# Moving the first products of four expert tiles into the attention stage of a two-layer gated transformer kernel, and making the tile lists in three parts

## The chip, the core and the metric

The kernel runs on one core of a Trainium2 chip (trn2). The metric is the device time of one execution in microseconds (us), and the figure of a kernel is the median of its runs. Engines are named as the profile names them: PE is TensorE (matrix products; PEld is its weight load), DVE is VectorE, ACT is ScalarE, POOL is GpSimd and SP is SyncE. Each works through its own queue of instructions in order, and an instruction that waits holds up all that stand behind it in that queue.

## What is computed

The reference is two layers, each of a cross-attention and a feed-forward part, on `x` of 4 batches of 512 tokens of width 256, all in float32. Only the last part matters for the change:

```python
x = x + tanh(g_xattn[0]) * attn0(layernorm(x), ctx)      # 16 heads of width 16, decay by distance
x = x + tanh(g_ffn[0])   * ffn0(layernorm(x))            # 256 -> 1024 -> 256, weights made ternary
x = x + tanh(g_xattn[1]) * attn1(layernorm(x), ctx)      # 16 heads, relu of q, k, v
x = x + tanh(g_ffn[1])   * ffn1(layernorm(x))
# ffn1, for h of 2048 tokens:
expert_idx = argmax(h @ W_router)                        # one of 4 experts for each token
hidden = gelu(h @ W1[expert_idx] + b1[expert_idx])       # 256 -> 1024
y = layer_norm(hidden @ Wo + bo + h) * ln_gamma + ln_beta
```

## The kernel before

**Attention.** A unit is one tile of 128 rows of one head group (four heads). There are 32 head groups (2 layers x 4 batches x 4) and so 128 units. In each unit PE makes four score products `pm` whose row maxima DVE takes (`maxima`, L504), six units ahead (`LEAD`), and four products `psc` of keys with shifted queries that ACT turns into exponentials (`weights`, L519). Each is a 32 x 128 by 32 x 512 product; four of them stand beside each other in the array. Every fourth unit PE multiplies the exponentials of a head group with the values (`weighted`, `po`, L547), and two units later it turns the maxima (`pmT`) and the last output (`pn`), which DVE divides and adds to `x`. All results of PE pass through eight PSUM banks that are handed out in turn (`bank_psum`): a product waits until the product eight places before it was read out by ACT or DVE.

**What fills the units.** Everything else of a layer is cut into jobs that stand in chains: a job has a cost in us of PE and a gap in units to the one before, and a chain has a first and a last unit. `slot(u)` runs after the scores of unit u: it takes due jobs, and others as long as their cost fits into `SLOT` = 3.1 us. Jobs are the projections of the next batch (`project`, `prepare`), the first feed-forward part (`ffn0`) and `route(b)`: the norm of the batch, its rows to a DRAM buffer `rows_d` (two DMAs on SP), the router's product `plT`, one-hot choice and the rank of each token within its expert (`ranks`, `prk`).

**The expert part** works on 19 tiles of 128 rows that hold tokens of one expert each. `dispatch(second)` makes a list: from ranks and counts DVE computes the place of each token (`lists`, `token_places`, `by_tile`), makes selection matrices (`picked`, `sel`, 128 x 512), and `gathered` multiplies them on PE (`pid_d`, L881: for each token tile a 128 x 128 weight load and a product of 9 or 10 columns) to get the token index of each row. The result goes to `get`, `put` and `wrow`, the index lists of the DMAs. The first list covers three batches and 9 tiles (`T_FULL`) and is made in the last units of attention; the second covers the rest and 10 tiles, and is made between the first tiles.

For a tile j, `fetch_rows` and `fetch_weights` (L918, L930) gather its rows and its 1 MB of expert weights by indirect DMAs that POOL issues. `turn_tile` (`ptx`, L1040) transposes the rows, ACT or DVE copies them to `xs`. `hidden_tile` (`pg`, L1101) makes the first product in two halves and ACT applies gelu out of PSUM (L1107). `output_tile` (`pyf`, L1117) makes the second product, `norm_tile` is the layer norm on DVE with one power on POOL (L1132), and `put_tile` (L1144) writes the rows out with an indirect DMA from POOL.

Only tile 0 is turned in attention, in the last unit. After attention the order is written out by hand: `hidden_tile(0)`, `weighted` of the last head group, tile 1 turned, `divided` of the last group, the weights of tiles 2 and 3, the norm of the last batch, and then for each j `hidden_tile(j)`, `turn_tile(j + 1)`, `put_tile(j - 2)`, `output_tile(j - 1)`, `norm_tile(j - 1)` and the fetches of tile j + 3. `early` and `late` name the steps of the last batch's routing and of the second list that stand between.

Of the kernel before, what the change touches and what calls it, by code (L numbers as in the profile page):

```python
# [19 lines left out]
P = 128  # L20
# [12 lines left out]
T_FULL = 9  # L33
T_ALL = TT + NE - 1
LEAD = 6
# [9 lines left out]
def flamingo_kernel(ctx: ExitStack, tc: tile.TileContext, t: dict, out: bass.AP):  # L45
# [727 lines left out]
    def dispatch(second):  # L773

        tiles = (TT, T_ALL - T_FULL) if second else ((B - 1) * NT, T_FULL)
        K, T = tiles
        j0 = T_FULL if second else 0
        nm = f"d{int(second)}"
# [7 lines left out]

        def lists():
# [3 lines left out]
            if second:  # L791
                nc.vector.tensor_tensor(left, count[:, K, :], taken, ALU.subtract)
            else:
                nc.vector.tensor_scalar(left, count[:, K, :], float(1 - P), None, ALU.add)
# [10 lines left out]
            nc.vector.tensor_reduce(ends, part, AX.X, ALU.add)  # L805
            first = ends[:, 0:NE]
            if second:
                first = small([NE], "first")
                nc.vector.tensor_tensor(first, ends[:, 0:NE], taken, ALU.subtract)
            else:  # L810
                nc.vector.tensor_scalar(ends, ends, float(P * T), None, ALU.min)
                nc.vector.tensor_tensor(taken, ends[:, 1 : NE + 1], ends[:, 0:NE], ALU.subtract)
            st.update(ends=ends, first=first)

        def token_places():
# [5 lines left out]
            if second:  # L821
                nc.vector.tensor_tensor(
                    ok, at, across(ends[:, 0:NE].unsqueeze(1), K, NE), ALU.is_ge
                )
            else:
                nc.vector.tensor_tensor(
                    ok, at, across(ends[:, 1 : NE + 1].unsqueeze(1), K, NE), ALU.is_lt
                )
            nc.vector.tensor_tensor(ok, ok, onehot[:, 0:K, :], ALU.mult)
# [5 lines left out]
        def by_tile():  # L835

            ends, place1 = st["ends"], st["place1"]
            ge = small([TT, T_ALL - T_FULL + 1], "ge")[:, 0:K, 0 : T + 1]
# [4 lines left out]
            tid = small([TT, T_ALL - T_FULL], "tid")[:, 0:K, 0:T]  # L843
# [5 lines left out]
            st.update(tid=tid, row1=row1)  # L849

        def by_expert():

            ends = st["ends"]
            past = small([T_ALL - T_FULL, NE - 1], "past")[:, 0:T, :]
# [4 lines left out]
            ex = small([T_ALL - T_FULL], "ex")[:, 0:T]  # L859
# [5 lines left out]
        def picked(k0):  # L865
            def run():
                pool, tag, bufs = (act, "oT", 2) if second else (wts, "xg", 4)
                sel = pool.tile([P, 4, P], F32, tag=tag, name=f"sel_{nm}{k0}", bufs=bufs)
# [8 lines left out]
        def gathered(k0):  # L877
            def run():
                pid = bank_psum(f"pid_{nm}{k0}")[:, 0:T]
                for k in range(4):  # L880
                    nc.tensor.matmul(  # L881
                        pid, lhsT=st["sel", k0][:, k, :], rhs=st["tid"][:, k0 + k, :],
                        start=(k == 0), stop=(k == 3),
                    )
                if k0 == 0:
                    st["pid"] = small([T_ALL - T_FULL], "pid")[:, 0:T]
                    nc.vector.tensor_copy(st["pid"], pid)
                else:
                    nc.vector.tensor_tensor(st["pid"], st["pid"], pid, ALU.add)
                if k0 + 4 == K:  # L890

                    nc.vector.tensor_scalar(
                        get[:, j0 : j0 + T], st["pid"], 1.0, -1.0, ALU.max, ALU.add
                    )
                    none = small([T_ALL - T_FULL], "none")[:, 0:T]
                    nc.vector.tensor_scalar(
                        none, st["pid"], 0.0, float(2 * B * S), ALU.is_equal, ALU.mult
                    )
                    nc.vector.scalar_tensor_tensor(
                        put[:, j0 : j0 + T], st["pid"], -1.0, none, ALU.add, ALU.add  # L900
                    )

            return run

        return (
            [(lists, 0, 0), (token_places, 0, 0), (by_tile, 0, 0)],
            [(picked(k), 0, int(k == 0)) for k in range(0, K, 4)],
            [(by_expert, 0, 1)],
            [(gathered(k), 1.0, int(k == 0)) for k in range(0, K, 4)],
        )  # L910

# [3 lines left out]
    def fetch_rows(j):  # L915
        have = (B if j >= T_FULL else B - 1) * S
        xg[j] = wts.tile([P, 2 * D], F32, tag="xg", name=f"xg{j}", bufs=4)
# [6 lines left out]
    def fetch_weights(j):  # L924

        if j % 5 < 2:
# [7 lines left out]
        )  # L934

# [26 lines left out]
    for layer in range(2):  # L962
# [21 lines left out]
    fetches = [  # L984
        (lambda j=j, f=f: f(j), 0, 0)
        for f, j in (
            (fetch_rows, 0), (fetch_weights, 0), (fetch_rows, 1), (fetch_weights, 1), (fetch_rows, 2),
            (fetch_rows, 3),
        )
    ]  # L990
    for b in range(B - 1):
        u0 = first_unit(1, b + 1)
        if b < B - 2:
            chain(route(b), u0 + 4, u0 + 13)
        else:
            heads, *rest = dispatch(False)
            heads[0] = (heads[0][0], 0, 0)
            chain([*route(b), *heads, *sum(rest, []), *fetches], u0 + 2, n_units - 5)
# [36 lines left out]
    xs, hs, ys = {}, {}, {}  # L1035

    def turn_tile(j):
# [231 lines left out]
```

## Time and profile before

| what | value |
|---|---|
| runs | 866.21, 863.21, 866.26 us; median 866.21 us |
| profiled execution, its own time | 865.25 us |
| its span, first to last instruction | 863.2 us, 13527 instructions |
| PE, DVE, ACT, POOL busy | 832.9, 555.2, 418.2, 271.7 us |
| mean granted TensorE clock | 0.985 |
| start of the last product with the values (`po`), end of the last `pyf` | 705.43 us, 852.84 us |

The profile is one execution; times in it count from its first instruction. It gives groups of equal instructions with their total, the chain of work that ended last followed back from the end, the order of instructions in time, and for chosen stretches the busy time of each engine with the granted clock of PE. Ends of products are modelled and they overlap, so a busy PE need not be at its peak: what a product costs is read from the start of one group of products to the start of the next. Each float32 product is recorded twice, so `x32` is 16 products.

### The profile page before, as it was taken

What the parts mean: (1) busy time and instruction counts of PE and PEld (TensorE: products, weight loads), DVE (VectorE), ACT (ScalarE), POOL (GpSimd) and SP (SyncE); (2) the same over time, 40 slices, a digit from 0 to 9 for tenths busy, and PEclk for the clock granted to TensorE, in tenths of its full rate; (3) what the DMA queues carried; (4) which work ended last, traced back from release to release, by engine and by line L of the source; (5) the groups of instructions that cost most, each with busy time, mean ns of one, the idle gap of its engine ahead of it and who ended that gap; (6) DMA issues with size and microseconds to landing.
All of it is one profiled execution on the core that took longest, in us unless ns stands there. A gap on an engine that the chain in (4) does not pass through costs nothing.

```text
span 863.2 us, 13527 instructions
## 1 busy us (share of the span) xinstructions
PE 832.9 (96%) x5222; PEld 472.6 (55%) x5222; DVE 555.2 (64%) x1192; ACT 418.2 (48%) x876; POOL 271.7 (31%) x435
## 2 busy tenths in 40 slices
PE   6999999999999999999999999999999999999995
PEld 3444444435463346445554445644444558999994
DVE  6778778766857784768646865577777615644443
ACT  2475565553555452655445563357566353233331
POOL 5536455524342422311100120012002035445542
PEclk9999999999999999999999999999999799999998
DMA  9100000000001000000000010001001046556650
GB/s 315 60 1 1 1 1 2 1 1 0 2 13 25 1 1 0 26 1 1 1 1 25 1 50 1 1 1 50 1 1 49 1 147 226 165 173 201 196 190 14
DMA packets 17775, 42.01 MB, mean 49 GB/s; under 512 B 2158, under 2 KB 12144, under 8 KB 15280
## 3 DMA queue, kind: packets, MB, share of 16 engines
q0 software_dynamic: 5168, 27.08, 9.5%
q1 hardware_dynamic: 12128, 13.54, 4.7%
q8 instruction: 41, 0.67, 0.3%
q10 hardware_dynamic: 416, 0.54, 0.2%
q14 instruction: 22, 0.18, 0.1%
HBM read 34.86 MB, written 6.68 MB: 48 GB/s over the span
## 4 chain that ended last, share of the span: by engine, by line
PE 74%; DVE 9%; issue 8%; POOL 5%; DMA 2%; ACT 1%; POOLq 0%; ACTq 0%; DVEq 0%
PE pm L490 15%; PE po L547 13%; PE psc L490 13%; PE ph L660 7%; PE py_f L375 7%; PE pk L447 4%; PE pva L416 4%; DVE m L504 4%; PE pq L447 3%; PE pmT L561 2%; PE py_wo L375 2%; DMA out_dram<-y,put 2%; POOL out_dram L1144 2%; POOL wg L930 2%; POOL rstd_y L1132 1%
## 5 line engine op out<-in xcount | busy, mean ns | idle before, releaser
L504 DVE TENSOR_REDUCE m<-pm 128x1 f32<-128x512 f32 x512 | 316.6, 682 | 106.3 <-PE psc L490 103.5
L519 ACT ACTIVATE p<-psc 128x512 f32<-128x512 f32 x512 | 267.6, 602 | 164.3 <-PE psc L490 161.1
L490 PE MATMUL psc<-q,k 32*128 32x512 f32 x1024 | 286.6, 635 | 2.1 <-DVE m L504 1.9
L490 PE MATMUL pm<-k,q 32*128 32x512 f32 x1024 | 266.8, 618 | 2.6 <-DVE m L504 1.7
L522 POOL TENSOR_TENSOR p<-p,dec 128x256 f32<-128x256 f32 x128 | 93.4, 734 | 179.1 <-ACT p L519 179.1
L490 PEld LDWEIGHTS pm<-k,q 32*128 32x128 f32 x1024 | 95.7, 185 | 87.7 <-issue 51.4
L490 PEld LDWEIGHTS psc<-q,k 32*128 32x128 f32 x1024 | 108.6, 186 | 55.5 <-issue 25.2
L547 PE MATMUL po<-p,v 128*32 128x512 f32 x1024 | 117.0, 597 | 1.9 <-DVE m L504 1.9
L1107 ACT ACTIVATE ha<-pg,wg 128x128 f32<-128x128 f32 x152 | 43.2, 369 | 89.1 <-PE pg L1101 83.3
L547 PEld LDWEIGHTS po<-p,v 128*32 128x32 f32 x1024 | 31.8, 110 | 83.5 <-issue 62.6
L1101 PE MATMUL pg<-xs,wg 128*128 128x128 f32 x608 | 71.2, 276 | 1.4 <-DVE xn_f L356 1.4
L1101 PEld LDWEIGHTS pg<-xs,wg 128*128 128x128 f32 x608 | 70.5, 192 | 3.3 <-issue 1.7
L1117 PE MATMUL pyf<-wo,ha 128*128 128x256 f32 x304 | 68.6, 379 | 0.0
L615 POOL TENSOR_TENSOR x<-x,o 128x256 f32<-128x256 f32 x14 | 10.2, 729 | 174.8 <-DVE o L608 142.9
L1117 PEld LDWEIGHTS pyf<-wo,ha 128*128 128x128 f32 x304 | 56.4, 190 | 6.8
L660 PE MATMUL ph<-xTf,w1q 128*128 128x512 f32 x128 | 60.0, 605 | 0.0
L553 ACT COPY oT<-po 128x512 f32<-128x512 f32 x32 | 18.7, 585 | 80.3 <-PE po L547 80.3
L375 PE MATMUL py_f<-w2q,h 128*128 128x256 f32 x256 | 57.2, 382 | 0.0
L375 PEld LDWEIGHTS py_f<-w2q,h 128*128 128x128 f32 x256 | 48.1, 190 | 9.3 <-DVE m L504 3.0
L1121 DVE TENSOR_TENSOR y<-y,pyf 128x256 f32<-128x256 f32 x19 | 8.0, 421 | 53.8 <-PE pyf L1117 53.5
L447 PE MATMUL pk<-cT,wk 128*128 128x512 f32 x68 | 35.1, 641 | 7.3 <-DMA cT<-in_ctxT_dram 7.3
L660 PEld LDWEIGHTS ph<-xTf,w1q 128*128 128x128 f32 x128 | 22.6, 190 | 30.4 <-issue 18.1
(204 smaller groups left out, 797.8 us busy)
## 6 DMA issues: line engine op xcount, KB each, us to landing
x<-in_x_dram SPq DMA_DIRECT2D x4, 512.0 KB, 8.6
rows_d<-xn_f SPq DMA_DIRECT2D x4, 512.0 KB, 3.0
rows_d<-x SPq DMA_DIRECT2D x4, 512.0 KB, 3.5
cT<-in_ctxT_dram SPq DMA_DIRECT2D x3, 512.0 KB, 9.6
w1q<-in_w_dram SPq DMA_DIRECT2D x1, 1024.0 KB, 8.8
w2q<-in_w_dram SPq DMA_DIRECT2D x1, 1024.0 KB, 11.2
wo<-in_wo_dram SPq DMA_DIRECT2D x2, 512.0 KB, 3.8
rows<-in_rows_dram SPq DMA_DIRECT2D x1, 640.0 KB, 9.1
```

Of the source, the lines that this page charges most:

```text
L375: nc.tensor.matmul(py[:, n, :], lhsT=operand(c, n0 + n), rhs=w[:, c, :], start=(c == 0), stop=(c == chunks - 1),)
L416: nc.tensor.matmul(pv[:, ts(n, D)], lhsT=cT[b][:, c, ts(n0 + n, P)], rhs=wv[:, c, :], start=(c == 0), stop=(c == NC - 1),)
L447: nc.tensor.matmul(pp, lhsT=attn_w[layer][w][:, c, ts(tt, P)], rhs=src[:, c, :], start=(c == 0), stop=(c == NC - 1),)
L490: nc.tensor.matmul(out_, lhsT=lhs[r, ts(n, P)], rhs=rhs[r, :], start=True, stop=True)
L504: nc.vector.tensor_reduce(m[:, n, 2 * pair + i, r : r + 1], pm[i], AX.X, ALU.max)
L519: nc.scalar.activation(p[:, i, :], psc[i], AF.Exp, scale=SCALE)
L522: nc.gpsimd.tensor_tensor(d, d, dec.unsqueeze(1).to_broadcast([P, 2, P]), ALU.mult)
L547: nc.tensor.matmul(po[i * HP : (i + 1) * HP, :], lhsT=v_sb[b % 2][0][:, kt, c0 : c0 + HP], rhs=ps_exp[NT * s + kt, i // 2][:, i % 2, :], s ...
L660: nc.tensor.matmul(ph, lhsT=w1q[:, c, ts(f, P)], rhs=st["xT"][:, c, :], start=(c == 0), stop=(c == NC - 1),)
L1101: nc.tensor.matmul(ph[:, f, :], lhsT=w[:, c, ts(f2 * NF // 2 + f, P)], rhs=xs[j][:, c, :], start=(c == 0), stop=(c == NC - 1),)
L1107: nc.scalar.activation(ha[:, f, :], ph[:, f, :], AF.Gelu, bias=wg[j][:, NC * FF + fa : NC * FF + fa + 1],)
L1117: nc.tensor.matmul(py, lhsT=hs[j, f // 4][:, f % 4, :], rhs=wo1[f // 4][:, f % 4, :], start=(f == 0), stop=(f == NF - 1),)
```

## The change

There are now three lists instead of two (`LISTS`): two batches and tiles 0 to 4, three batches and tiles 5 to 8, four batches and tiles 9 to 18. The first is made as soon as batch 1 is routed, in the third batch's units of layer 1 and the first of the fourth's; the second in the last six units of attention; the third between tiles as before. Four tiles (`T_AHEAD`) have rows and weights fetched within attention, are turned there and have their first product made there, all but the second half of tile 3. These steps are jobs of a chain, with costs 0.3 and twice 1.75. Their results are only copied out of PSUM, by ACT for tiles 0 to 2 and by DVE for tile 3; the bias is kept by a copy on POOL, and gelu runs after attention from SBUF to SBUF (`activated`). The rows of tiles 0, 1 and 2 are fetched a second time for the residual.

The token indices are no longer gathered by products with 128 x 128 weights. `collected` takes the index matrix (padded to 32 columns, set to zero on POOL) as weights and the selection as the moving side, four token tiles at a time in column strips of the array. The result is copied by ACT, transposed by PE and summed by DVE over the four strips (`tokens`). In a list after the first, DVE has up to five more small instructions.

After attention the order is a queue: second half of tile 3, gelu of tile 0, the last `weighted`, tile 4 turned, last `divided`, the norm of the last batch, then the fetches of rows 5, 3, 6, 7 and weights 5, 6, 7 on POOL. On PE follow the first product of tile 4, the turning of tile 5, the second products of tiles 0 to 3 with the last batch's routing between, the first product of tile 5, and then second product of j and first product of j + 2 in turn. Tile 9, the first of the last list, is turned just before the second product of tile 8, and tile 10 is turned right before its own first product.

```diff
-T_FULL = 9
+LISTS = ((2, 0), (3, 2 * NT - NE + 1), (4, 3 * NT - NE + 1))
+T_LIST = T_ALL - LISTS[-1][1]
+T_AHEAD = 4
...
+            tid = space("tid").rearrange("p (k w) -> p k w", w=HP)
+            nc.gpsimd.memset(tid, 0.0)
...
-        def gathered(k0):
-            def run():
-                pid = bank_psum(f"pid_{nm}{k0}")[:, 0:T]
-                for k in range(4):
-                    nc.tensor.matmul(
-                        pid, lhsT=st["sel", k0][:, k, :], rhs=st["tid"][:, k0 + k, :],
-                        start=(k == 0), stop=(k == 3),
-                    )
...
+        def collected():
+
+
+            pT = bank_psum(f"pidT_{nm}")[:, 0:P]
+            for k in range(K):
+                nc.tensor.matmul(
+                    pT[k % 4 * HP : (k % 4 + 1) * HP, :], lhsT=st["tid"][:, k, :],
+                    rhs=st["sel", k - k % 4][:, k % 4, :], start=(k < 4), stop=(k >= K - 4),
+                )
+            st["pT"] = const.tile([P, P], F32, tag="dec", name=f"pT_{nm}")
+            nc.scalar.copy(st["pT"], pT)
+
+        def tokens():
+            pp = bank_psum(f"pid_{nm}")[:, 0:P]
+            nc.tensor.transpose(pp, st["pT"], ident)
+            pid = small([T_LIST], "pid")[:, 0:T]
+            nc.vector.tensor_reduce(
+                pid, pp.rearrange("p (i t) -> p t i", i=4)[:, 0:T, :], AX.X, ALU.add
+            )
...
+    def turn_tile(j):
...
+        copy = nc.vector.tensor_copy if j == T_AHEAD else nc.scalar.copy
+        copy(xs[j], pt.rearrange("p (c n) -> p c n", c=NC))
+
+    def hidden_half(j, f2):
...
+        if j < T_AHEAD:
+            ha = wts.tile([P, S], F32, tag="h", name=f"ha{j}{f2}", bufs=8)
+            if f2 == 0:
+                biases[j] = sml.tile([P, NF], F32, tag="b1", name=f"b1_{j}")
+                nc.gpsimd.tensor_copy(biases[j], b1)
...
+        if j < T_AHEAD:
+            (nc.scalar.copy if j < T_AHEAD - 1 else nc.vector.tensor_copy)(ha, ph)
+        else:
+            activated(j, f2, ph)
...
+            turn_0, *rest_0 = tile_steps(0)
+            ahead = chain(
+                [
+                    *route(b), *dispatch(0), step(fetch_rows, 0), step(fetch_weights, 0),
+                    step(fetch_rows, 1), step(fetch_weights, 1), step(fetch_rows, 2),
+                    step(fetch_rows, 3), (turn_0[0], turn_0[1], 2), *rest_0, step(fetch_rows, 4),
+                    step(fetch_weights, 2, gap=1), *tile_steps(1), step(fetch_rows, 0),
+                    step(fetch_weights, 3, gap=1), *tile_steps(2), step(fetch_rows, 1),
+                    step(fetch_weights, 4, gap=1), *tile_steps(3)[:2],
+                ],
+                u0 + 3, n_units - 1,
+            )
...
+            routed = chain(route(b), u0 + 2, u0 + 9)
+            chain(dispatch(1), n_units - LEAD, n_units - 1, routed)
...
-    hidden_tile(0)
+    hidden_half(T_AHEAD - 1, 1)
+    fetch_rows(2)
+    for f2 in range(2):
+        activated(0, f2)
     weighted(last)
-    turn_tile(1)
+    turn_tile(T_AHEAD)
     divided(last)
...
+    steps = {
+        ("o", 1): [turn3], ("o", 2): [products3], ("o", 3): [logits3],
+        ("h", 5): [ranks3, lists, token_places, by_tile], ("o", 4): [*sels, by_expert],
+        ("h", 6): [collected], ("o", 5): [tokens],
     }
...
+    first = LISTS[-1][1]
+    queue = [("h", 4), *(("o", j) for j in range(4)), ("h", 5)]
+    for j in range(4, T_ALL - 2):
+        queue += [("o", j), ("h", j + 2)]
+    queue.remove(("o", first - 1))
+    queue.insert(queue.index(("h", first)), ("o", first - 1))
+    queue += [("o", T_ALL - 2), ("o", T_ALL - 1)]
+    for j in (5, 3, 6, 7):
+        fetch_rows(j)
+        if j > 3:
+            fetch_weights(j)
+    for kind, j in queue:
+        if kind == "h":
+            for f2 in range(2):
+                hidden_half(j, f2)
+            if j + 1 < T_ALL and j + 1 != first:
+                turn_tile(j + 1)
+        else:
+            if j + 1 == first:
+                turn_tile(first)
+            if j < 3:
+                for f2 in range(2):
+                    activated(j + 1, f2)
+            output_tile(j)
+            norm_tile(j)
+            if j > 0:
+                put_tile(j - 1)
```

## The prediction, made before the changed kernel ran

> **What bounds the kernel now.** I read the page first: PE is busy for 832.9 of 863.2 us, so only what PE does, or waits for, near the end can matter. Then the granted clock in short stretches, the order of instructions in time, and the DMA table. The stretches (columns: us; PE, PEld, DVE, ACT, POOL busy; clock; DMA share; GB/s):
>
> ```profile
> 675.00:680.00 5.00, 3.13 (x12) 1.17 (x8) 4.62 (x18) 2.65 (x6) 0.00 (x0) 0.96 0.01 2
> 680.00:685.00 5.00, 5.00 (x18) 2.08 (x16) 4.61 (x11) 1.19 (x2) 0.73 (x1) 0.50 0.00 0
> 685.00:690.00 5.00, 5.00 (x28) 4.99 (x24) 0.34 (x2) 2.06 (x4) 0.00 (x0) 0.50 0.00 0
> 690.00:695.00 5.00, 5.00 (x34) 1.58 (x37) 0.58 (x4) 2.06 (x4) 3.28 (x3) 0.67 0.36 80
> ```
>
> PE runs at half clock from about 679.6 to 693.3 (0.96 and 0.67 give the ends), just where the first list is made. The order in time says why:
>
> ```profile
> 677.99 2.48 DVE L504 TENSOR_REDUCE m<-pm 128x1 f32<-128x512 f32 x4
> 678.73 2.43 PE L490 MATMUL psc<-q,k 32*128 32x512 f32 x4 [1.87 <-DVE m L504]
> 680.39 1.88 DVE L869 TENSOR_TENSOR sel_d<-from_one,row_d 128x512 f32<-128x512 f32 x3
> 685.01 5.29 PE L881 MATMUL pid_d<-tid_d,sel_d 128*128 128x9 f32 x24
> ```
>
> DVE did 3.8 us of list arithmetic (674.18 to 677.99) ahead of the maxima, PE ran out of PSUM banks, and the index products then took 5.22 us at half clock. After attention the bound is PE alone, with one DMA wait at tile 2:
>
> ```profile
> 709.77 0.66 PE L598 MATMUL pn<-ident,oT 128*128 128x128 f32 x4 [0.34 <-ACT oT L553]
> 712.73 1.02 POOL L930 DMA_INDIRECT wg<-in_w1e_dram,wrow  x1 [12.02 <-DVE st_f L321]
> 717.41 0.20 POOL L336 TENSOR_TENSOR rstd_f<-rstd_f,fix_f 128x4 f32<-128x4 f32 x1
> 719.04 3.81 PE L1101 MATMUL pg<-xs,wg 128*128 128x128 f32 x32 [1.36 <-DVE xn_f L356]
> ...
> 838.53 0.38 PE L1040 MATMUL ptx<-ident,xg 128*128 128x128 f32 x2
> 838.75 3.62 PE L1117 MATMUL pyf<-wo,ha 128*128 128x256 f32 x16
> 842.20 3.73 PE L1101 MATMUL pg<-xs,wg 128*128 128x128 f32 x32
> 845.77 7.07 PE L1117 MATMUL pyf<-wo,ha 128*128 128x256 f32 x32
> ```
>
> The DMA table gives the time from issue to landing (last column, median us):
>
> ```profile
> xg<-rows_d,get POOLq DMA_INDIRECT x19, 3.6
> wg<-in_w1e_dram,wrow POOLq DMA_INDIRECT x19, 6.6
> ```
>
> The wait at 719.04 is for the weights issued at 712.73, which land 6.0 us later; the norm's last row only ends beside it. Start to start, a tile in the steady part is 3.57 (`pg`), 0.22 (`ptx`), 3.46 (`pyf`): 7.25 us with no gap. Moving 3.57 us of PE work into attention gains only what attention hides; PE's work as a whole stays. So I add up two parts: attention from the `po` of head group 27 on, and everything behind the last `po`.
>
> **Part one: attention, before 88.4 us** (617.0 to 705.4). Cut at each `po`, five stretches A to E take 18.1, 17.5, 16.6, 23.1, 13.2. A bare stretch needs 3.57 (`po`) + 4 x 1.93 (scores of four units) + 1.0 (`pmT`, `pn`) = 12.3 on PE; those with jobs show about 14.2 plus the jobs, the rest being waits for DVE and ACT.
> - Ahead of A: the first list is 12 small instructions on DVE (2.6 us by the rows 674.18 to 676.80) before the maxima of a unit. `po` needs the bank of the first maximum: 4.8 us after `prk` where it was 3.2. **+1.6.**
> - A: two selections (0.63 each) and `by_expert` (0.85) delay the next maxima, 0.9; eight strip products have their nearest row in `plT` (same shape, 0.57), then a transpose and 0.7 on DVE; partly beside DVE's backlog. **20.1, +2.0.**
> - B: tile 0. `ptx` 0.25 and two halves of 1.79 lie largely beside DVE's 3.3 us of division and statistics (PE idled 1.03 there, inside 8.2 us for two units). **18.0, +0.5.**
> - C: tile 1 and half of tile 2: 3 x 1.79 + 2 x 0.25. Here `pg` stands right behind `ptx`, so PE waits for ACT's copy `xs` (0.4), which is queued behind four exponentials (2.1) and, at first, `xTf` (0.6). Before, ACT finished `xTf` 8.6 us into C; `xs` is then ready at 9.2 and PE, free at 7.25, waits 2.0; at tile 2 some 1.0. **24.1, +7.5.** Behind the waiting `pg` stand all scores.
> - D: half of tile 2 and half of tile 3. 3.57 + 1.95 (scores) + 0.45 (`prk`) + 1.8 + 1.0 (scores without maxima) + 1.0 + 0.25 + 1.2 (wait for `xs`) + 1.8 + 1.95 + 0.8 (a bank that DVE empties behind the second list) = **15.8, -7.3.** The maxima are over by now, so the list's arithmetic no longer holds PE, and the clock should stay whole.
> - E: 3.57 + 4 units at 1.0, less one that is in D, + 0.85 (12 strip products by `plT`) + 0.5 (`pn`) + 0.5 (wait for `pT` on ACT and transpose) + 1.8 (last half): **10.2, -3.0.** It had 1.4 us of slow clock in it.
>
> Sum +1.3: 13.6 us of moved products cost almost nothing net, because D and E lose the wide index products, the stall and the half clock.
>
> The prefetches are covered: weights 2 are issued about 8.8 us into C behind POOL's addition (which ended at 661.3) and land by 16.5, used at 20; if that cover fails, scores wait, some 1 to 3 us. Six more DMA issues of 1.3 us and the bias copies sit on POOL, which was busy for 5.5 of the 40 us from 640; POOL's additions to `x` behind them have 15 us before anyone reads. The weights' 4 MB and three more row gathers meet DMA engines that stood at a share of 0.00 to 0.08.
>
> **Part two: behind the last `po`, before 147.4 us** (705.43 to 852.84).
> - `pn` waits for ACT's copy `oT`, now behind table load (1.28) and eight gelu (2.3): 5.2 after `po` starts instead of 4.3. With `pn` and tile 4's `pg`, PE is at 9.3.
> - The new wait: PE's next is `ptx` of tile 5, whose rows POOL fetches only behind the last batch's norm. Before, `pn` to the last statistic was 4.5 us (714.24), and POOL's norm took 2.5 (715.11 to 717.61). Row gather and wake-up 4.0: ready at 5.2 + 4.5 + 2.5 + 4.0 = 16.2. **PE stands 7.0 us.** Behind it all second products are queued. From below: nothing else feeds `ptx`, so under 5.5 is excluded unless the gather lands in 2 us; from above 8.5, with a 7.2 us landing excluded by idle DMA engines.
> - Four `pyf` with `pt_f` (0.9) and `plT` (0.6): to 31.8. Tile 5 and `ptx`: 35.7. `prk` waits for DVE (norm of y 3.3, choice 1.0): 37.0. `pyf`, `pg`, `ptx`: 44.2.
> - The strip products of list three wait for all four selections, behind list arithmetic (5.3 after `prk`, as at 739.68 to 745.02), a norm (3.8) and 4 x 0.63: 48.5, **3.7 us of stall**. Before, the selections were spread over two tiles and the 32 records of `pid_d` cost 3.5.
> - Remaining: 13 `pyf`, 12 `pg`, 11 `ptx`, and `pyf` 5: 93.7. Tile 10 is turned right before its `pg`: gelu of half a tile and the copy stand between, **1.6**. End at 143.8.
> - Clock. The row: half clock came after 1.87 us of waiting in light work, and once (near 648.9) after 1.03; the 1.36 before 719.04 brought none. The Trainium skill ("TensorE: Matmul & The Clock Gate", "What's actually happening") says that an idle window of about 3.4 us is needed, and one busy window to come back. By the rule only the 7 us stall is punished, once the clock is back after up to 3.4 to 6.8 us: 2 us, and C's waits are free. By the row, the 3.7 us stall (1.2) and perhaps C's 2.0 (half of 1.7) count as well. I take the row: 4.0 us.
>
> Total part two 147.0 with the 3.2 that belongs here: -0.4. The last writes are as before (10.4 us behind the last `pyf`).
>
> **Sum.** 865.25 (profiled execution) + 1.3 - 0.4 + 0.8 (clock in C) = 867.0; the median of the runs lies 1.0 above that execution, so 867 to 868. I put 867.2, the likeliest: no difference to speak of. A measurement here can tell about 0.5% (4.3 us) from no change, so "same" is 861.9 to 870.5.
>
> **Rivals.**
> 1. Faster: the new stalls are shorter than I think, the jobs as well hidden. If PE's 7.0 us wait were 4, C's waits 1 instead of 3, and the clock cost 1.5: 3 + 2 + 2.5 = 7.5 off, 859.5. For it: A to E had 21 us of waits in which to hide; against: `ptx` stands behind a POOL norm that the trace times well. 22%.
> 2. Slower: the half clock. Jobs that wait for `xs` in C and D leave light stretches; the trace held half clock for four windows once PE had idled 1.87 us, as long as light work followed. Three windows of 3.4 us in C to E, each costing up to 1.7, make +5.1: 872.2. It decides from two waits over 1.9 us that follow each other within 7 us. Against: a `pg` half is dense work and lies between. 20%.
> 3. The move doesn't hide: D and E recover only the slow products (5.2 to 0.85), not the stall, since lists on DVE still stop PE's banks; +5 to +8, 872 to 875. 9%.
> 4. The forecast: 49%, own range 863 to 871.
>
> Ends of the unknowns: stall 5.5 to 8.5, C 22 to 26, clock 1.5 to 6. The range for 8 in 10 is 859.5 to 873. Faster by over 0.5%: 0.22; within: 0.49; slower: 0.29.
>
> **What would show it.** In the profile after: `ptx` of tile 5 idle some 7 us, released by a DMA or POOL; clock 0.5 behind it; no half clock where `pid_d` stood; C longer by 7, D and E shorter by 10. Wrong if the last `po` starts more than 4 us away from 707, or if that idle is under 4.

## The result, and the profile after

The changed kernel takes 872.33 us (median of six runs, 870.33 to 873.45), the kernel before 865.18 us (six runs beside it, 862.0 to 866.26). The ratio is 1.0088, with a 95% interval of 1.0066 to 1.011: slower by about 7 us. The profiled execution took 872.11 us, with a span of 870.4.

Cut at each start of `po`, as in the prediction, the two profiles compare so (us; the last two columns are experiments from below, all mends with early turns, and column strips alone with tile 0 turned later):

| stretch | before | forecast | after | mends | strips |
|---|---|---|---|---|---|
| first instruction to A | 617.0 | 618.6 | 618.9 | 617.15 | 616.0 |
| A | 18.1 | 20.1 | 20.1 | 20.1 | 18.1 |
| B | 17.5 | 18.0 | 19.1 | 19.3 | 17.8 |
| C | 16.6 | 24.1 + 0.8 | 25.8 | 21.45 | 18.1 |
| D | 23.1 | 15.8 | 16.5 | 14.8 | 17.8 |
| E | 13.2 | 10.2 | 11.1 | 11.1 | 9.1 |
| last `po` to the end of the last `pyf` | 147.4 | 147.0 | 146.2 | 137.2 | 147.3 |
| to the end | 10.4 | 10.4 | 12.7 | 10.7 | 10.7 |

The stretches of 5 us of the changed kernel (columns as in the prediction: us; PE, PEld, DVE, ACT, POOL busy; clock; DMA share; GB/s):

```profile
665.00:670.00 5.00, 3.30 (x17) 3.07 (x16) 0.94 (x2) 2.08 (x5) 3.04 (x3) 0.72 0.76 229
...
685.00:690.00 5.00, 5.00 (x45) 1.95 (x37) 1.98 (x5) 2.21 (x5) 0.00 (x0) 1.00 0.01 3
690.00:695.00 5.00, 4.36 (x35) 3.24 (x34) 2.94 (x11) 3.25 (x7) 0.00 (x0) 1.00 0.00 0
...
720.00:725.00 5.00, 0.08 (x1) 0.00 (x0) 2.31 (x7) 1.14 (x4) 3.24 (x7) 1.00 0.00 0
725.00:730.00 5.00, 2.26 (x7) 1.93 (x8) 0.93 (x2) 1.56 (x6) 4.05 (x4) 0.52 0.92 278
```

The half clock that stood at 680 to 693 is gone (1.00 in the second and third row). It has come up in two other places: in C (0.72), and behind a PE that does nothing from 720 to 725 (0.08 us busy) and then works at 0.52. The order of instructions in time of the same kernel names both waits:

```profile
667.13 3.68 PE L996 MATMUL pg<-xs,wg 128*128 128x128 f32 x16 [1.70 <-ACT xs L977]
...
705.06 0.43 PE L912 MATMUL pidT_d<-tid_d 128*32 128x128 f32 x8
705.30 0.62 PE L912 MATMUL pidT_d<-sel_d,tid_d 128*32 128x128 f32 x16
...
711.51 3.64 PE L551 MATMUL po<-p,v 128*32 128x512 f32 x32
...
723.58 1.16 POOL L950 DMA_INDIRECT xr<-rows_d,get  x1 [0.66 <-issue]
...
727.74 0.66 PE L974 MATMUL ptx<-ident,xr 128*128 128x128 f32 x2 [7.66 <-issue]
728.19 8.11 PE L1178 MATMUL pyf<-wo,ha 128*128 128x256 f32 x28
```

The strip products of the second list now start at 705.06 and PE is on to the next scores at 705.85; the wide form they replace took 5.2 us. The wait of 7.66 us is ahead of `ptx` of tile 5. "issue" only says that the profile shows no releaser; the row gather that POOL issues at 723.58, behind the last batch's norm, is what `ptx` reads. All second products (`pyf`) stand behind it.

Two more losses lie where the forecast had none. The first is on DVE, some 40 us ahead of A (order in time of the changed kernel):

```profile
577.02 0.40 DVE L325 BATCH_NORM_STATS2 st_f<-x 128x6 f32<-128x256 f32 x1
577.45 0.18 DVE L326 BATCH_NORM_AGGREGATE mv_f<-st_f 128x2 f32<-128x6 f32 x1
577.55 0.39 DVE L325 BATCH_NORM_STATS2 st_f<-x 128x6 f32<-128x256 f32 x1
...
578.79 3.64 PE L551 MATMUL po<-p,v 128*32 128x512 f32 x32 [1.57 <-DVE m L508]
```

These are `route(1)`'s statistics. Its chain starts at `u0 + 3` where it was `u0 + 4`, so the first two of them stand right behind the statistics of the attention's own norm in the same unit, ahead of the maxima, and `po` waits 1.57 us (0.52 before) for a bank that DVE's maxima free. This and the next head group took 1.06 and 0.56 us longer.

The second is at the very end (order in time, POOL alone):

```profile
855.70 0.73 POOL L1193 TENSOR_TENSOR rstd_y<-var_y,power 128x1 f32<-128x1 f32 x1 [4.84 <-DVE var_y L1192]
856.63 1.03 POOL L1205 DMA_INDIRECT out_dram<-y,put  x1 [0.20 <-issue]
859.40 0.73 POOL L1193 TENSOR_TENSOR rstd_y<-var_y,power 128x1 f32<-128x1 f32 x1 [1.73 <-DVE var_y L1192]
860.33 1.03 POOL L1205 DMA_INDIRECT out_dram<-y,put  x1 [0.20 <-issue]
863.54 0.98 POOL L1205 DMA_INDIRECT out_dram<-y,put  x1 [2.19 <-issue]
```

`put_tile(j - 1)` now comes behind `norm_tile(j)`, where it came ahead of `output_tile(j)`. So the writes of tiles 17 and 18 stand one behind the other, and the last is issued 2.19 us after its predecessor's issue has ended, 5.80 us behind the end of the last `pyf`; before, it was 3.84 (the same two writes there):

```profile
852.98 1.02 POOL L1144 DMA_INDIRECT out_dram<-y,put  x1 [1.45 <-DVE y L1139]
856.68 1.02 POOL L1144 DMA_INDIRECT out_dram<-y,put  x1 [1.45 <-DVE y L1139]
```

Between tiles, the strip products of the third list wait for DVE's selections, as forecast, though for 2.1 us and not for 3.7 (order in time of PE):

```profile
760.12 0.94 PE L912 MATMUL pidT_d<-sel_d,tid_d 128*32 128x128 f32 x16 [2.11 <-DVE sel_d L899]
...
762.19 3.72 PE L1178 MATMUL pyf<-wo,ha 128*128 128x256 f32 x16
```

### The profile page after: what moved, and what is told of

It reads as the page before. It is cut to its first block, busy times and chain, and to the rows that moved or that the text cites. A ratio compares the mean times of both kernels' runs of the same rounds, so it can differ in the third digit from the quotient of the medians.

```text
span 870.4 us, 13598 instructions
## 1 busy us (share of the span) xinstructions
PE 825.7 (95%) x5241; PEld 464.3 (53%) x5241; DVE 563.8 (65%) x1218; ACT 422.4 (49%) x886; POOL 278.9 (32%) x446
## 5 line engine op out<-in xcount | busy, mean ns | idle before, releaser
L494 PE MATMUL psc<-q,k 32*128 32x512 f32 x1024 | 280.4, 624 | 0.2 <-DVE h L672 0.2
L494 PE MATMUL pm<-k,q 32*128 32x512 f32 x1024 | 263.1, 617 | 1.3 <-ACT q L481 0.9
L494 PEld LDWEIGHTS pm<-k,q 32*128 32x128 f32 x1024 | 93.1, 185 | 84.1 <-issue 50.1
L996 PE MATMUL pg<-xs,wg 128*128 128x128 f32 x608 | 74.1, 280 | 4.8 <-ACT xs L977 4.1
L619 POOL TENSOR_TENSOR x<-x,o 128x256 f32<-128x256 f32 x14 | 10.2, 728 | 189.7 <-DVE o L612 128.3
L1178 PE MATMUL pyf<-wo,ha 128*128 128x256 f32 x304 | 70.6, 388 | 0.0
L1009 ACT ACTIVATE ha<-pg,wg 128x128 f32<-128x128 f32 x120 | 34.2, 368 | 71.3 <-PE pg L996 69.4
## 6 DMA issues: line engine op xcount, KB each, us to landing
w2q<-in_w_dram SPq DMA_DIRECT2D x1, 1024.0 KB, 11.1
```

The lines of the kernel that those rows point to most:

```text
L494: nc.tensor.matmul(out_, lhsT=lhs[r, ts(n, P)], rhs=rhs[r, :], start=True, stop=True)
L996: nc.tensor.matmul(ph[:, f, :], lhsT=w[:, c, ts(f2 * NF // 2 + f, P)], rhs=xs[j][:, c, :], start=(c == 0), stop=(c == NC - 1),)
L1009: nc.scalar.activation(ha[:, f, :], (ha if src is None else src)[:, f, :], AF.Gelu, bias=biases[j][:, fa : fa + 1],)
L1178: nc.tensor.matmul(py, lhsT=hs[j, f // 4][:, f % 4, :], rhs=wo1[f // 4][:, f % 4, :], start=(f == 0), stop=(f == NF - 1),)
```

## Experiments

The theory at the start: the 7 us are the sum of separate waits of PE, each made by where a step stands in a queue, and each can be taken away by itself. The first rival: DVE (or ACT) is the limit where PE waits, so that a wait taken away comes back behind the next product. The second: the wait ahead of `ptx` of tile 5 covers POOL and DVE work that PE would meet next.

**Tile 5 turned later.**

```diff
-            if j + 1 < T_ALL and j + 1 != first:
+            if j + 1 < T_ALL and j + 1 != first and j > T_AHEAD:
...
-        ("o", 1): [turn3], ("o", 2): [products3], ("o", 3): [logits3],
+        ("o", 1): [turn3], ("o", 2): [products3, lambda: turn_tile(5)], ("o", 3): [logits3],
```

> The changed kernel with one step moved: tile 5 is turned after the second product of tile 2 and the router's product, no longer right behind tile 4's first product. Theory (the stall in front of tile 5's transposition costs its 7.8 us and some 3 us of half clock behind it): nothing else is late, the products of tiles 0 to 3 run at once, and the time falls by 8 to 11 us, to 861 to 864. Rival (POOL is the real limit there: seven gathers at 1.3 us stand ahead of the power of tile 0's norm, DVE waits for that power in order, and the half of the last batch's transposed rows that DVE copies stands behind two such norms): a new stall of 5 to 7 us in front of the router's product plT, and only 2 to 5 us are gained, 867 to 870.

Measured: 871.6 us (ratio 1.0079, 1.0049 to 1.011). The wait had gone from `ptx`, and a new one of the same size stood ahead of the last batch's router product (order in time of this kernel):

```profile
731.69 0.99 POOL L962 DMA_INDIRECT wg<-in_w1e_dram,wrow  x1 [0.31 <-issue]
732.70 0.59 POOL L1193 TENSOR_TENSOR rstd_y<-var_y,power 128x1 f32<-128x1 f32 x1
733.33 0.22 DVE L1195 SCALAR_TENSOR_TENSOR fix_y<-rstd_y,var_y 128x1 f32<-128x1 f32 x1 [5.90 <-issue]
...
738.06 0.68 DVE L372 COPY xTf<-pt_f 128x512 f32<-128x512 f32 x1
...
738.79 0.66 PE L738 MATMUL plT<-xTf,wr 128*32 128x128 f32 x8 [7.39 <-DVE xTf L372]
```

Read upwards: `plT` waits for DVE's half of `xTf`, which stands in DVE's queue behind the norms of tiles 0 and 1; tile 0's norm waits 5.90 us for POOL's power; and the power stands behind seven indirect fetches, 723.29 to 732.68, 1.3 us each. My theory fell as stated: turning the tile later is not enough. The rival had named this place, though of its gain of 2 to 5 us only 0.7 came. It also says what to try next.

**And the fetches split.** On top of the edit above:

```diff
-    for j in (5, 3, 6, 7):
-        fetch_rows(j)
-        if j > 3:
-            fetch_weights(j)
+    fetch_rows(5)
+    fetch_rows(3)
+    fetch_weights(5)
+    later = {1: (fetch_rows, 6), 2: (fetch_weights, 6), 3: (fetch_rows, 7), 4: (fetch_weights, 7)}
...
                 put_tile(j - 1)
+            if j in later:
+                later[j][0](later[j][1])
```

> Tile 5 is turned after the last batch's router product, as in the run before of that kind, and only rows 5, rows 3 and weights 5 are fetched ahead of the queue; rows 6, weights 6, rows 7, weights 7 are issued one each after the norms of tiles 1 to 4. Theory (the stall of 7.39 us ahead of plT was GpSimd's: seven indirect fetches of 1.3 us each stood ahead of tile 0's power, and VectorE, in order, held the copy of xTf behind it): the stall falls below 1 us, one or both half-clock windows behind it go: 862 to 866 us. Rival (the wait is due to something else in the last batch's chain, its rows written to DRAM or its statistics, and only changes its place): another wait of 4 us or more between the last po and tile 8, 869 to 872 us.

Measured: 864.25 us (ratio 0.9994, 0.998 to 1.0008), as fast as the kernel before. The same place in time:

```profile
727.67 0.59 POOL L1193 TENSOR_TENSOR rstd_y<-var_y,power 128x1 f32<-128x1 f32 x1
...
733.75 0.43 PE L738 MATMUL plT<-xTf,wr 128*32 128x128 f32 x8 [2.21 <-DVE xTf L372]
```

The power comes 5 us earlier, and 2.21 us of the wait are left (I had expected under 1): DVE still does the norms of two tiles ahead of the copy. From the last `po` to the last `pyf` it is 139.5 us, 6.7 less than in the changed kernel. So this stall, with the half clock that follows it, is the largest single loss, and its cause is the place of two steps in two queues.

**Route(1) one unit later.**

```diff
-                u0 + 3, n_units - 1,
+                u0 + 4, n_units - 1,
```

> The changed kernel with route(1) starting one attention unit later again, as before the change. Theory (the 1.6 us that units 93 to 100 took longer came from the four bn_stats of route(1), which stand on VectorE one unit earlier): 1.6 us less than the changed kernel, about 870.3 us. Rival (these units grew for another reason, the step that stands in them is only moved on): 871.5 to 872.5 us, with the same growth in other units.

Measured: 869.61 us (ratio 1.0056, 1.0042 to 1.0071). The `po` of 578.79 has its old wait again, and A starts at 616.98, to 0.01 us where it does in the kernel before:

```profile
577.43 3.64 PE L551 MATMUL po<-p,v 128*32 128x512 f32 x32 [0.52 <-DVE m L508]
```

So this term is 1.6 us, as the theory had it. The median fell by more than that, 2.8 by the ratios, but the two intervals overlap. In the profile a second difference is C: 24.15 us where the changed kernel has 25.8, with PE's waits for `xs` unchanged (4.1 us in three waits over the whole kernel in both, one of them tile 10's). The clock makes it (in both kernels C has the wait of 1.70 us; first the changed kernel, cut at the edges of its half clock, then this one):

```profile
663.77:667.18 3.41, 1.55 (x11) 1.04 (x11) 2.17 (x4) 3.31 (x8) 2.54 (x2) 1.00 0.44 154
667.18:670.60 3.42, 3.42 (x16) 3.42 (x16) 0.00 (x0) 0.00 (x0) 1.02 (x2) 0.50 0.73 199
```

```profile
660.00:665.00 5.00, 3.31 (x26) 1.73 (x22) 3.08 (x5) 5.00 (x11) 2.35 (x1) 1.00 0.48 157
665.00:670.00 5.00, 4.83 (x39) 3.53 (x40) 1.69 (x3) 2.25 (x6) 1.21 (x2) 1.00 0.78 238
```

In the changed kernel the wait lies whole within one window of 3.41 us, in which PE is busy for 1.55, and the next window runs at half clock; here no window goes slow. The same wait costs 1.6 us more or nothing. That the wait is spread over two windows here is the likely reason; the trace does not show a window's edges where the clock stays whole. In this profile the part behind the last `po` is longer by as much (147.9 us for 146.2), so C's gain is no part of what the edit is worth.

**The copy of `xs` on DVE.**

```diff
-    copy = nc.vector.tensor_copy if j == T_AHEAD else nc.scalar.copy
+    copy = nc.vector.tensor_copy if j <= T_AHEAD else nc.scalar.copy
```

> The changed kernel with the copies of the transposed rows of tiles 0 to 3 on DVE, where they were on ACT. Theory (in stretches C and D the first product waits behind ACT's exponentials for its operand): PE's waits there of 2.1, 1.1 and 1.5 us fall to about 0.6 each, the half clock that follows the first goes too, C and D shorten by 3 to 5 us together, 867 to 869. Rival (DVE, with the maxima, is the fuller engine, and the copies hold the maxima up): C and D shorten by under 1 us or grow.

Measured: 877.38 us (ratio 1.0142), 5 us worse than the changed kernel. C is 24.7 us (25.8), but D is 22.4 (16.5):

```profile
697.16 0.20 DVE L860 TENSOR_REDUCE place_d<-at_d 128x12 f32<-128x48 f32 x1
697.28 0.41 DVE L977 COPY xs<-ptx 128x256 f32<-128x256 f32 x1
697.79 3.75 PE L996 MATMUL pg<-xs,wg 128*128 128x128 f32 x16 [5.31 <-issue]
```

Here the copy for tile 3 stands behind sixteen instructions of the second list. So where DVE makes a list, ACT is the better engine for the copy; the next run tests whether the fault is that PE asks for it at once.

**Tiles turned one half earlier.**

```diff
-                    step(fetch_rows, 3), (turn_0[0], turn_0[1], 2), *rest_0, step(fetch_rows, 4),
-                    step(fetch_weights, 2, gap=1), *tile_steps(1), step(fetch_rows, 0),
-                    step(fetch_weights, 3, gap=1), *tile_steps(2), step(fetch_rows, 1),
-                    step(fetch_weights, 4, gap=1), *tile_steps(3)[:2],
+                    step(fetch_rows, 3), (turn_0[0], turn_0[1], 2), rest_0[0], turn_1, rest_0[1],
+                    step(fetch_rows, 4), step(fetch_weights, 2, gap=1), rest_1[0], turn_2, rest_1[1],
+                    step(fetch_rows, 0), step(fetch_weights, 3, gap=1), rest_2[0], turn_3, rest_2[1],
+                    step(fetch_rows, 1), step(fetch_weights, 4, gap=1), half_3,
```

> The changed kernel with tiles 1, 2 and 3 turned between the two halves of the tile before, so that ScalarE's copy of xs lies beside a half's 1.8 us of products. Theory (in stretches C and D TensorE waits 2.1, 1.1 and 1.5 us for that copy, and the first of these waits also brings the half clock at 667): C and D together 3 to 5 us shorter: 867 to 869 us. Rival (in C the scores wait for VectorE's maxima and ScalarE's exponentials anyway, so the waits only move from the products to the scores): C and D together within 1 us, 870.5 to 872.5 us.

Measured: 866.71 us (ratio 1.0019, 1.001 to 1.0028), 6 us less than the changed kernel. C is 21.5 us and D 14.8, together 6.0 less (expected 3 to 5). In the order in time of this kernel `ptx` stands between other products, and no `pg` waits:

```profile
665.10 1.95 PE L996 MATMUL pg<-xs,wg 128*128 128x128 f32 x16
666.88 0.38 PE L974 MATMUL ptx<-ident,xg 128*128 128x128 f32 x2
667.19 0.70 PE L494 MATMUL pm<-k,q 32*128 32x512 f32 x2
...
670.86 2.05 PE L996 MATMUL pg<-xs,wg 128*128 128x128 f32 x16
```

C has no half clock here, which is 1.6 of the 6.0. The rival, that DVE and ACT hold the scores back anyway, is out: these waits were PE's own.

**The last write.** One write moved: tile 17's comes right behind its norm, not behind tile 18's.

```diff
-            if j > 0:
+            if 0 < j < T_ALL - 1:
                 put_tile(j - 1)
+            if j == T_ALL - 2:
+                put_tile(j)
```

> The changed kernel with tile 17's rows written right behind its own norm, as in the kernel before, and not behind tile 18's norm. Theory (the last two writes wait for one another's landing, 2.2 us that the new order puts on the end): the last write starts 2 us earlier against the last product, the time falls by 2.0 to 2.3 us, to 870. Rival (the wait belongs to the write itself, a queue or a buffer): no change, 872.3.

Measured: 869.71 us (ratio 1.0049, 1.0033 to 1.0064), 2.6 less than the changed kernel. The size agrees, yet the profile (of this kernel's slowest run, 872.72 us) shows only a third of it at the end: the last write is issued 5.04 us behind the last `pyf` (5.80 in the changed kernel). Where the other 1.8 us of the median come from is not shown.

```profile
857.98 1.03 POOL L1205 DMA_INDIRECT out_dram<-y,put  x1 [0.20 <-issue]
860.91 1.00 POOL L1205 DMA_INDIRECT out_dram<-y,put  x1 [1.91 <-DVE var_y L1192]
861.92 0.58 POOL L1193 TENSOR_TENSOR rstd_y<-var_y,power 128x1 f32<-128x1 f32 x1
```

Tile 17's `y` was ready at 858.93 and its write is issued at 860.91, 2.9 us after the start of tile 16's; tile 18's power stands behind it on POOL. So the wait has moved up by one tile. This trace names no releaser for it, but the kernel before has the same wait with its releaser, the landing of the write before (issued at 834.62, landed at 839.50):

```profile
840.30 1.04 POOL L1144 DMA_INDIRECT out_dram<-y,put  x1 [3.05 <-DMA out_dram<-y,put]
```

That a write waits for its predecessor's landing is therefore the likely cause here too. In the kernel before, writes land 2.1 to 7.1 us after their issue starts, in the median 5.1; the last but one took 2.47. Only when the writes of tiles 16 and 17 are both issued ahead of the next tile's `output_tile`, as before the change, is the distance 3.84 us again (in the run with all mends and early turns below: last `pyf` ends at 841.11, last write at 844.95).

**All mends together**, that is tile 5 later, fetches split, the last write, route(1) later:

> The run with tile 5 turned later and split fetches, with the last writes as before the change and route(1) one unit later. Theory (the terms are independent and add): 2.3 + 1.6 = 3.9 us less than that run: 858 to 862 us, below the kernel before by 3 to 7. Rival (the end is set by writes that follow one another, or the half clock falls on another stretch): less than 2 us below that run.

Measured: 861.76 us (ratio 0.997, 0.9956 to 0.9985), 2.5 less by the medians than with tile 5 and the fetches alone, 2.1 by the ratios, whose intervals overlap: less than the sum of 3.9, and too near the rival's 2 to put it out. This last write is the half mend just shown.

**The third list spread out**, with those mends:

```diff
-        ("h", 5): [ranks3, lists, token_places, by_tile], ("o", 4): [*sels, by_expert],
-        ("h", 6): [collected], ("o", 5): [tokens],
+        ("h", 5): [ranks3, lists, token_places, by_tile], ("o", 4): [*sels[:2], by_expert],
+        ("h", 6): sels[2:], ("o", 5): [collected], ("h", 7): [tokens],
...
                 hidden_half(j, f2)
+                if j == first and f2 == 0:
+                    turn_tile(j + 1)
```

with the fetches of tile 9 moved behind `tokens`.

> All mends, and the third list spread out: two of its selections after tile 4's output, two after tile 6's first product, its products after tile 5's output, its tokens after tile 7's first product; tile 10 turned between the two halves of tile 9. Theory (the waits of 2.3 and 2.1 us at the third list's products and the 1.4 us ahead of tile 10's first product end on work that is one step too late for TensorE): 2 to 5 us less than the run with all mends: 855 to 859 us. Rival (rows 9 come later by one tile and TensorE waits for them, or the waits only move): within 1 us of the run with all mends, or above.

Measured: 861.47 us (ratio 0.9958, 0.9944 to 0.9972): as fast as without it. In its profile (of its fastest run, 858.4 us) the waits for the selections (2.1 us) and for tile 10's `xs` were gone, and a new one had come:

```profile
754.25 3.81 PE L996 MATMUL pg<-xs,wg 128*128 128x128 f32 x32 [2.67 <-DMA wg<-in_w1e_dram,wrow]
```

**All of it with early turns**, weights 9 fetched behind `by_expert`, and the last two writes issued ahead of `output_tile`:

> All mends of the run with the third list spread out, with the early turns as well, weights 9 fetched right behind by_expert instead of with rows 9, and the last two writes issued ahead of the second products of tiles 17 and 18, as before the change. Theory (each wait is TensorE's own and adds): 2.7 us of wait for weights 9, 1.5 at the last writes, 3 to 5 in C and D, off the 861 us of the run with the list spread out: 852 to 856 us, the fastest of all. Rival (some of these waits cover for VectorE's or ScalarE's work and only move): 858 to 861 us.

Measured: 853.53 us (ratio 0.988, 0.9862 to 0.9898): in the range expected, the fastest until then, though one term of the sum was wrong. The wait for weights stayed:

```profile
744.53 1.10 POOL L962 DMA_INDIRECT wg<-in_w1e_dram,wrow  x1 [0.30 <-issue]
```

```profile
750.58 3.81 PE L996 MATMUL pg<-xs,wg 128*128 128x128 f32 x32 [2.99 <-DMA wg<-in_w1e_dram,wrow]
```

I had put it down to tile 9. It is tile 7, whose weights my own split had moved behind the norm of tile 4, 3 us before PE is ready for them (744.53 and 747.59); until then PE's wait for the selections had probably hidden that. The last run moves the four fetches up by one tile:

```diff
-    later = {1: (fetch_rows, 6), 2: (fetch_weights, 6), 3: (fetch_rows, 7), 4: (fetch_weights, 7)}
+    later = {0: (fetch_rows, 6), 1: (fetch_weights, 6), 2: (fetch_rows, 7), 3: (fetch_weights, 7)}
```

> The run with all mends and early turns, with rows 6, weights 6, rows 7 and weights 7 issued after the norms of tiles 0 to 3 instead of 1 to 4. Theory (the 3.0 us ahead of a first product there are a wait for weights 7, which were issued 3 us before TensorE needed them): the wait goes, 2.5 to 3.5 us less than that run, about 850.5 us. Rival (with rows 6 on GpSimd's queue behind tile 0's power, tile 1's norm is late and the copy of xTf with it, so the wait for xTf of 2.2 us grows by as much): 852.5 to 854.5 us.

Measured: 850.98 us (ratio 0.9831, 0.9812 to 0.9851), faster than the kernel before by 1.7% and the fastest of all. Against the run before it is 2.5 us less by the medians, 4.2 by the ratios. The rival is out: PE's wait for `xTf` stays at 2.24 us, though `prk` waits 0.5 longer. PE goes from the strip products into tile 7 without a wait:

```profile
747.64 0.43 PE L912 MATMUL pidT_d<-sel_d,tid_d 128*32 128x128 f32 x8 [0.17 <-DVE sel_d L899]
747.99 3.84 PE L996 MATMUL pg<-xs,wg 128*128 128x128 f32 x32
```

**Column strips alone**, in the kernel before: `collected` and `tokens` in place of `gathered`, two lists, nothing moved into attention.

```diff
-            [(gathered(k), 1.0, int(k == 0)) for k in range(0, K, 4)],
+            [(collected, 0.9, 1), (tokens, 0.3, 1)],
...
-        5: [*sels[:2], by_expert], 6: sums[2:],
+        5: [*sels, by_expert], 6: sums[:1],
...
-    late = {3: [logits3], 5: [*sums[:2], *sels[2:]]}
+    late = {3: [logits3], 6: sums[1:]}
```

> The kernel before with one part of the change alone: the token indices by strip products, copy, transposition and sum, the two lists kept; the four selections of the second list are now made together ahead of it. Theory (wide index products were dear because they ran as light work at half clock): the stretch D shortens by 3 to 4.5 us; behind the last po the second list costs up to 2 us more than before, since its selections come in one piece; together 861.5 to 864.5 against 865.2. Rival (the index products only filled a time in which PE would have waited for DVE or ACT): D unchanged within 1 us, the time 865 to 867.

Measured: 861.44 us (ratio 0.9967, 0.9954 to 0.998). D is 5.3 us shorter than before, and its half clock lasts from 678.7 to 685.6, half as long as in the kernel before (679.6 to 693.3), though DVE's wait ahead of it is the same (1.95 us); so the wide products had kept the clock down for longer, and the rival is out. But E is 6.0 longer:

```profile
696.12 0.41 PE L1041 MATMUL ptx<-ident,xg 128*128 128x128 f32 x2 [2.00 <-DMA xg<-rows_d,get]
...
700.47 6.47 PE L1102 MATMUL pg<-xs,wg 128*128 128x128 f32 x32 [2.87 <-DMA wg<-in_w1e_dram,wrow]
```

The fetches of tile 0 hang on `tokens`, and PE arrives there sooner than they do: two waits, and `pg` at half clock (6.47 us for a 3.8 us group). Putting the last `po` between needs three lines:

```diff
-        if u == n_units - 1:
-            turn_tile(0)
...
-    hidden_tile(0)
+    turn_tile(0)
     weighted(last)
+    hidden_tile(0)
```

> The run with column strips alone on the kernel before, with tile 0 turned after the last scores and the last po ahead of tile 0's products. Theory (there TensorE stood 2.4 us ahead of ptx of tile 0, because its rows are fetched behind the tokens, and half clock from 699.2 to 706.0 followed): 3 to 5 us less: 856.5 to 858.5 us. Rival (the last po waits for ScalarE's last exponentials, and the half clock falls elsewhere): 860.5 to 862.5 us.

Measured: 856.78 us (ratio 0.9903, 0.9885 to 0.9921). Both waits are gone, and E takes 9.1 us (C's 18.1 in the table, 16.6 before, holds a longer half clock: 648.1 to 654.9, where the kernel before has 648.9 to 652.3):

```profile
696.48 0.44 PE L1041 MATMUL ptx<-ident,xg 128*128 128x128 f32 x2
696.85 3.64 PE L547 MATMUL po<-p,v 128*32 128x512 f32 x32
700.55 3.81 PE L1100 MATMUL pg<-xs,wg 128*128 128x128 f32 x32
```

So the strips are the part of the change that pays by itself, alone (0.9967) and more with tile 0 turned later; the later turn without strips was not run. What the move into attention is worth beyond them stays open: the best run with the move is 0.9831, this one 0.9903. By the two profiles the former spends 7.0 us more up to the last `po` and 12.5 less behind it, but it also has a third list, spread out between the tiles, that this one has not.

## Why the prediction was right or wrong

The measured time lies inside the range, at its upper edge, but the likeliest case, no difference, is not what happened, and the forecast's own range of 863 to 871 ends below it. By the prediction's own sign part one was wrong as well: the last `po` starts at 711.51, 4.5 us from 707. The stall, its place and its half clock were foreseen; that the total holds is in part luck, since terms of 7.8 us too low stand against 2.7 too high. The forecast of the profiled execution was 867.0 us, and it took 872.1. The 5.1 us are these terms:

- **A step that the sum did not contain: the statistics of `route(1)`, +1.6.** I costed the first list, and not the shift of its chain by one unit, although of a moved step every instruction counts. The run with the old start takes A's start back to 616.98.
- **"The last writes are as before": false, +2.3.** The diff showed `put_tile(j - 1)` behind `norm_tile(j)`. I read the order of PE in it and not that of POOL.
- **Ahead of A, +1.6 forecast, 0 measured.** DVE's list arithmetic did not reach the maxima that `po` waits for; less these, A starts where it did.
- **B, 1.1 too low.** Tile 0's products take 4.2 us (0.37 + 1.88 + 1.98, start to start), and only 2.6 of them found a wait to lie in; I had hidden 3.3.
- **C, 0.9 too low: the mechanism was right.** `pg` behind `ptx` waits for ACT's `xs`, 2.0 and 1.0 forecast. PE's waits were 1.70 and 0.69 (the 2.1, 1.1 and 1.5 us in two of the expectations run from the start of `ptx` to the start of `pg`, with the 0.4 of `ptx` in them). Without half clock C is 24.15 to 24.18 us in four runs that keep the order of C; I had said 24.1. With its one half-clock window it is 25.8, where I had put in half a window's price (0.8).
- **D and E, 0.7 and 0.9 too low.** The wait for `xs` in D was right (1.16, forecast 1.2). Half of a first product among scores takes 1.98 us start to start where I had put 1.8, which is 0.4 of D and 0.2 of E; and three units of scores in E take 3.9 us where I had put 3.0. That D and E shrink by 7 and 3 us for the loss of the wide products, the stall and the half clock was right in kind (-6.6 and -2.1).
- **The stall ahead of tile 5's `ptx`: 7.0 forecast, 7.66 measured.** `ptx` starts 16.2 us behind the last `po`, as forecast, but by two errors that cancel: `pn` comes at 4.3 and not 5.2, since ACT's table load and gelu ran beside `po` (711.38 to 715.13), and from the end of POOL's norm to `ptx` it is 4.8 and not 4.0. PE is ready 0.7 earlier than I had it. Half clock from 725.2 to 732.0 stands behind it.
- **Behind the last `po`, 0.8 too high.** The strip products of the third list start 48.6 us behind it (forecast 48.5). The half clock, some 2.1 us by estimate (half of the 4.3 us that PE works in it), seems only to have shortened the wait ahead of them, 2.1 for 3.7; I had added 3.2 for the clock on top. Against that, the strip products themselves, 2.1 us to the next `pyf`, stood nowhere in my sum.
- The start of the kernel adds 0.3, and the time outside the span is 0.3 shorter.

1.6 + 2.3 - 1.6 + 1.1 + 0.9 + 0.7 + 0.9 - 0.8 + 0.3 - 0.3 = 5.1.

**The rivals.** That the stalls are shorter did not hold. Half clock in C came once and not three times; its condition, two waits over 1.9 us within 7 us, was not met (1.70 and 0.69 us, 13 us apart), so it is chance that its 872.2 is near the time measured. That the move does not hide did not hold either: D and E did lose the stall. Against the forecast the kernel lost 3.9 us at two places outside the stretches that I had costed, and 3.6 in B to E, which I had costed too low.

**The forecast's "nothing else feeds `ptx`"** holds, but it took the order of PE's queue as given. Nothing forces tile 5 to be turned ahead of four ready second products; with the turn and the fetches moved, 7 us come back. A forecast of the change as written need not say so; one that asks what the change is worth should.

**The clock.** In the profiles half clock comes in stretches of 3.4 us (667.2 to 670.6), 6.8 (725.2 to 732.0) and 13.7 (679.6 to 693.3, before), so in windows of 3.4 us. A window with 1.55 us of work was followed by half clock. The rule of the Trainium skill that the prediction weighed ("TensorE: Matmul & The Clock Gate", "What's actually happening"), that an idle window of about 3.4 us is needed, would have left C free; the trace decides for the row with less, and C paid 1.6 us. The same section calls the window free-running, and that fits what two runs with one and the same wait showed (25.8 and 24.15 us for C).

## What to carry to other kernels

When work is moved to fill an engine's waits, go through every queue that the new order touches, to its first and last instruction: here the two largest unforeseen losses lay 40 us ahead of A and at the end of the kernel. Put a step with a dependent copy one product ahead of where its result is needed, and long fetch issues where nothing small stands behind them; the same change was 0.9% slower or 1.7% faster by such placements alone. A wait that is taken away uncovers the next one, so look at the profile again after each.

## What the runs showed of the hardware that was not expected

- Of two indirect writes whose data were ready close together, the second was issued only 2.9 to 3.2 us after the first; 3.7 us apart, in the kernel before, it waited only for its data. Where the trace names a releaser, it is the landing of the first (3.05 us of wait at 840.30 in the kernel before).
- POOL needs 1.3 us from one indirect fetch to the next. Seven in a row, in the run with tile 5 turned later, took it 9.4 us, held a 0.59 us power for 5.7 of them (its operand was there at 727.0), and PE, two queues further, for 7.39.
- One wait of 1.70 us was enough for a window of 3.4 us at half clock in one kernel, and not in another with the same wait.
